# SS2D selective scan: the copy of dt * x into PSUM moves from TensorE to ScalarE, and an order edge behind it is taken out

## The chip, the cores and the metric

The kernel runs on one core of a Trainium2 chip. Its engines work side by side, each on its own queue in order: TensorE (PE in the profile, with its weight loads as PEld), VectorE (DVE), ScalarE (ACT) and GpSimd (POOL); SyncE (SP) issues nearly all the DMAs. The metric is the device time of one launch in microseconds (us).

## The reference, cut to what matters

The network has four layers on eight images of 56 x 56 positions with 128 channels, all in float32. Layers 0, 2 and 3 are deformable convolution blocks, which the change doesn't touch. Layer 1 is a VSS block: layer norm, an input projection, a depthwise convolution, the selective scan in two dimensions (SS2D), and an output projection with an MLP. The scan is the part that matters:

```python
x0 = xb.reshape(B, Di, L)                       # Di = 256, L = 3136
x1 = xb.transpose(0, 1, 3, 2).reshape(B, Di, L)
xs = jnp.stack([x0, x1, x0[..., ::-1], x1[..., ::-1]], axis=1)   # 4 directions
...
dt = jax.nn.softplus(dt + dt_projs_b[None, :, :, None])
A = -jnp.exp(A_logs).reshape(K, Di, N)          # N = 16 states a channel

def step(h, t):
    dt_t, u_t, B_t, C_t = t
    h = h * jnp.exp(dt_t[..., None] * A) + (dt_t * u_t)[..., None] * B_t[:, :, None, :]
    y = jnp.einsum('bkdn,bkn->bkd', h, C_t)
    return (h, y)
```

So each of 256 channels has 16 states; each state is a linear recurrence over 3136 positions, with the decay exp(dt * A) and the input (dt * x) * B; the output is the sum over the states of h * C.

## The kernel before, in words

`Vss.scans` works through 128 steps: 8 images, 4 directions and 4 chunks of 784 positions (SC). A step has 32 units. A unit puts 32 channels (TC) times 4 states (TS) on the 128 partitions and 784 positions along the free dimension. The units of a step go by channel group cg (8 of them) and, within one, by state group sg (0 to 3); four units thus share one channel group, which the text calls a group. There are 4096 units and 1024 groups.

A group's tile dt holds two planes, dt and dt * x, each repeated over the 4 states; one DMA fetches it (`fetch_dt`, three buffers). A unit then takes these steps:

- `decay`: ScalarE makes dA = exp(dt * A) from plane 0 of dt, into PSUM (two buffers).
- `inputs`: u = (dt * x) * B. For sg 0, 1 and 2 VectorE does it, and reads dt * x from dtu, a copy in PSUM. For sg 3 (`on_pool`) GpSimd does it, straight from plane 1 of dt, into up.
- VectorE scans: h from dA and u (three buffers of h). ScalarE copies the last column of h to st, the state with which the next chunk starts.
- GpSimd multiplies h by C into hc (six buffers).
- `add_sums`: TensorE sums hc over the states into acc in PSUM, two units at a time and three units later. `open_sums` and `close_sums` start acc and take it out through ScalarE.

`spread` makes the copy dtu: two matmuls of 392 columns with an identity matrix. It is called once for each group, in the unit with sg 1, for the group after it. dtu has one buffer, of two PSUM banks, so that the copy for the next group waits until VectorE has made this group's third u. `spread` keeps its last matmul in `self.last_spread`, and `add_sums` issues its matmuls inside `issue_after(self.last_spread)`: an order edge, by which these sums come behind the last copy in TensorE's queue.

Between the units, work of other stages is fed in as generators, some pieces at each unit: `prepare` makes dt, B and C of the next step, `input_stage` makes the projection and convolution of the next image, and `output_stage` the output projection and MLP of chunks already scanned. They use TensorE, ScalarE, VectorE and GpSimd, with one PSUM bank named misc. The code names what is issued and in which order; a planner of the framework then arranges each engine's queue by the costs that it assumes, and the arrangement differs from the order of the calls. The order of instructions in each queue is fixed in the program.

Of the kernel before, what the change touches and what calls it, by code (L numbers as in the profile page):

```python
# [120 lines left out]
SH = SC // 2  # L121
# [11 lines left out]
TC, TS = 32, 4  # L133
NCG, NSG = DI // TC, NST // TS
# [855 lines left out]
class Vss:  # L990
# [309 lines left out]
    def scans(self):  # L1300
        nc, w = self.nc, self.w
# [33 lines left out]
        def spread(at, t):  # L1335

            s, (cg, sg) = state[at], order[t]
            ps = s["dtu", cg] = self.pdtu.tile([128, 2, 512], F32, name="dtu", tag="dtu")
            for b in range(2):
                last = nc.tensor.matmul(ps[:, b, :SH], lhsT=self.net.ident, rhs=s["dt", cg][:, 1, SH * b : SH * (b + 1)], start=True, stop=True)  # L1340
            self.last_spread = last.ins

        def decay(at, t):
            (i, k, c), s, (cg, sg) = steps[at], state[at], order[t]
# [26 lines left out]

        def add_sums(at, group):
            acc = state[at]["acc"]
            with self.tc.issue_after(self.last_spread):
                for (cg, sg), hc in group:
                    for b in range(2):
                        r = 64 * b + TC * (cg % 2)
                        nc.tensor.matmul(acc[r : r + TC, :SH], lhsT=w["sum"], rhs=hc[:, SH * b : SH * (b + 1)], start=False, stop=sg == NSG - 1)  # L1378

        def close_sums(at, t):  # L1380
            (i, k, c), acc, (h, r) = steps[at], state[at]["acc"], place(t)
# [12 lines left out]
            if t == NT - 1:  # L1394
                state[at] = None
                if k == 2:
                    tasks.extend(self.output_stage(i, e) for e in (2 * c + 1, 2 * c))

        spread(*units[0])
        decay(*units[0])  # L1400
        inputs(*units[0])
        st = ready = None
        group, late = [], deque()
        zeros = self.zeros()
        for now, (at, t) in enumerate(units):
# [31 lines left out]
            if now + 1 < len(units):  # L1437
                decay(*units[now + 1])
                if not on_pool(units[now + 1][1]):
                    inputs(*units[now + 1])  # L1440

                if sg == NSG - 3 and now + 3 < len(units):
                    spread(*units[now + 3])
# [6 lines left out]
            if c != (NSC - 1 if forward else 0):  # L1450
                last = SC - 1 if forward else 0
                nc.scalar.copy(st[:, t : t + 1], hh[:, last : last + 1])  # L1452
            hc = self.work.tile([128, SC], F32, name="hc", tag="hc", bufs=6)
            nc.gpsimd.tensor_mul(hc, hh, s["c", sg])  # L1454
            group.append((order[t], hc))
            if t % 2:
                late.append((now + 3, add_sums, (at, group)))
                group = []
                if t % (2 * NSG) == 2 * NSG - 1:
                    late.append((now + 5, close_sums, (at, t)))  # L1460
# [83 lines left out]
```

## Time and profile before

| what | value |
|---|---|
| time, median of the runs | 18467.62 us (18457.31 to 18490.28) |
| span of the profiled execution | 18479.8 us |
| scan stage, from the first scan to the last | 2366 to 13800 us, 11434 us |
| busy in the stage: PE, DVE, ACT, POOL | 8638, 10264, 7052, 10454 us |
| granted TensorE clock: whole span, stage | 0.826, 0.86 |

The profiled execution's own time is known by its span alone, from its first to its last instruction, which is 12 us above the median of the runs. In the profile, a line such as L1340 is a line of the kernel; `dtu<-dt,ident` names the tile that is written and those that are read; `<-` behind an idle time names who ended it. Each of these matmuls stands as two records, so one call of `spread` gives four. Busy shares are best read inside the stage, since before and behind it other layers run.

### The profile page before, as it was taken

The page shows a single profiled execution, that of the slowest core. Times are in us where ns is not written, and L with a number is a line of the kernel's source. Part 1 is how long each engine was busy: PE and PEld are TensorE (multiplying, and loading weights), DVE is VectorE, ACT ScalarE, POOL GpSimd, SP SyncE. Part 2 cuts the span into 40 slices and gives each one's busy share as a digit, 9 for nine tenths or more (in the row PEclk, how much of TensorE's full clock was granted, in tenths as well). Part 3 has the DMA queues.
Part 4 walks back from the last instruction along what each step waited for, and adds up shares of the span by engine and source line. Part 5 has one row for each costly group of instructions (what it writes and reads, how often), then busy time and mean ns, then how long its engine had stood idle before and what let it go on. Part 6 is the DMA issues. An engine that isn't in the chain of part 4 may idle for free. (4 is left out here: it accounts for less than half of the span.)

```text
span 18479.8 us, 257190 instructions
## 1 busy us (share of the span) xinstructions
PE 13780.6 (75%) x89795; PEld 6844.2 (37%) x89795; DVE 15510.8 (84%) x18797; ACT 11145.4 (60%) x20690; POOL 11801.5 (64%) x6462
## 2 busy tenths in 40 slices
PE   5777787678678778678778768767665888577777
PEld 4555422222222222222222222222224666455555
DVE  8888379988988988988988898898985887688886
ACT  4666565566566566566566656656554666456666
POOL 2221089998998998998998998899981111222221
PEclk7878888889889889889888888888886888677777
DMA  7777444444443444344343443443433777577777
GB/s 215 205 210 200 122 158 160 162 158 148 142 149 137 146 147 140 140 150 139 140 150 136 143 152 135 143 150 136 147 122 110 196 198 198 143 204 204 201 204 175
DMA packets 1341779, 2961.90 MB, mean 160 GB/s; under 512 B 91168, under 2 KB 892132, under 8 KB 1325836
## 3 DMA queue, kind: packets, MB, share of 16 engines
q1 hardware_dynamic: 1340460, 2945.21, 51.4%
q8 instruction: 718, 11.76, 0.3%
q14 instruction: 601, 4.92, 0.1%
HBM read 2243.88 MB, written 866.92 MB: 168 GB/s over the span
## 5 line engine op out<-in xcount | busy, mean ns | idle before, releaser
L1454 POOL TENSOR_TENSOR hc<-h,c 128x784 f32<-128x784 f32 x4096 | 7560.9, 1873 | 764.2 <-DVE h L1449 534.4
L1449 DVE TENSOR_TENSOR_SCAN h<-dA,st,u 128x784 f32<-128x784 f32 x3072 | 5569.9, 1838 | 316.2 <-ACT dA L1346 182.3
L1346 ACT ACTIVATE dA<-dt,v_A 128x784 f32<-128x784 f32 x4096 | 3742.8, 915 | 719.1 <-DVE h L1449 717.8
L1356 DVE TENSOR_TENSOR u<-dtu,b 128x784 f32<-128x784 f32 x3072 | 2875.7, 957 | 559.9 <-PE dtu L1340 555.5
L1378 PE MATMUL acc<-hc,v_sum 128*32 128x392 f32 x16384 | 3222.3, 552 | 105.8 <-POOL hc L1454 105.6
L1340 PE MATMUL dtu<-dt,ident 128*128 128x392 f32 x4096 | 2105.1, 642 | 1512.1 <-issue 1102.6
L736 POOL TENSOR_TENSOR ay<-hat,om 112x756 f32<-112x756 f32 (+2 forms) x192 | 525.8, 2738 | 2750.0 <-ACT hat L727 2346.6
L1449 DVE TENSOR_TENSOR_SCAN h<-dA,st,up 128x784 f32<-128x784 f32 x1024 | 1876.7, 1833 | 242.4 <-POOL hc L1454 176.7
L1352 POOL TENSOR_TENSOR up<-dt,b 128x784 f32<-128x784 f32 x1024 | 1900.3, 1856 | 132.1 <-DVE h L1449 110.8
L807 ACT COPY st<-pt 128x448 f32<-128x448 f32 (+1 forms) x2240 | 1177.8, 542 | 1216.4 <-PE pt L805 1210.1
L1452 ACT COPY st<-h 128x1 f32<-128x1 f32 x3072 | 581.7, 189 | 2159.0 <-DVE h L1449 2150.5
L1340 PEld LDWEIGHTS dtu<-dt,ident 128*128 128x128 f32 x4096 | 862.0, 235 | 2564.6 <-issue 1672.2
L775 DVE TENSOR_TENSOR win<-win,patch 112x252 f32 (+2 forms) x3456 | 1695.4, 503 | 124.4 <-DVE win L775 34.2
L805 PE MATMUL pt<-ident,sw 112*128 112x112 f32 (+2 forms) x8960 | 1609.7, 310 | 199.1 <-DMA sw<-skew 198.8
L1378 PEld LDWEIGHTS acc<-hc,v_sum 128*32 128x32 f32 x16384 | 769.8, 117 | 2488.2 <-issue 1675.4
L766 POOL MEMSET win<- 128x1820 f32 (+2 forms) x384 | 630.1, 1646 | 1466.2 <-DMA skew<-win 1159.6
L821 PE MATMUL yps<-st,xw 128*32 128x48 f32 (+5 forms) x35840 | 1077.7, 245 | 397.6 <-ACT st L807 394.8
L805 PEld LDWEIGHTS pt<-ident,sw 112*128 112x128 f32 (+2 forms) x8960 | 1119.5, 161 | 485.6 <-DMA sw<-skew 166.9
L772 DVE TENSOR_TENSOR patch<-ay,hat 112x756 f32<-112x756 f32 (+2 forms) x1152 | 1221.3, 1066 | 22.5 <-POOL ay L736 19.5
L821 PEld LDWEIGHTS yps<-st,xw 128*32 128x32 f32 (+2 forms) x35840 | 757.0, 126 | 825.9 <-ACT st L807 476.1
L1112 PE MATMUL misc<-xn,v_tap 128*128 128x448 f32 x2016 | 867.3, 574 | 96.5 <-ACT xn L1146 61.2
L725 ACT ACTIVATE hat<-om,taps 112x252 f32<-112x252 f32 x1280 | 755.7, 729 | 287.1 <-DVE patch L772 273.4
(165 smaller groups left out, 19517.2 us busy)
## 6 DMA issues: line engine op xcount, KB each, us to landing
dt<-dds SPq DMA_DIRECT2D x1024, 784.0 KB
b<-rows SPq DMA_DIRECT2D x512, 392.0 KB
c<-rows SPq DMA_DIRECT2D x512, 392.0 KB
dds<-dd SPq DMA_DIRECT2D x256, 784.0 KB
sw<-skew SPq DMA_DIRECT2D x224, 812.0 KB
sw<-skew SPq DMA_DIRECT2D x224, 672.0 KB
sw<-skew SPq DMA_DIRECT2D x224, 588.0 KB
xw<-table SPq DMA_DIRECT2D x224, 320.0 KB
```

The lines of the kernel that those rows point to most:

```text
L772: nc.vector.tensor_mul(patch[:n], bcast(a, 3, KX), bcast(b, 2, KY))
L775: self.last_add = nc.vector.tensor_add(to, to, patch[:n, NCB * p : NCB * (p + 1)]).ins
L805: last = nc.tensor.transpose(ps[:m, n * g : n * (g + 1)], sw[:n, g, p : p + m], self.net.ident[:n, :n])
L807: nc.scalar.copy(st[:m], ps[:m, : G * n])
L821: self.nc.tensor.matmul(yps[CG * g : CG * (g + 1), t0:t1], lhsT=xw[:m, k + part, CG * g : CG * (g + 1)], rhs=st[:m, at + t0 : at + t1], st ...
L1340: last = nc.tensor.matmul(ps[:, b, :SH], lhsT=self.net.ident, rhs=s["dt", cg][:, 1, SH * b : SH * (b + 1)], start=True, stop=True)
L1346: nc.scalar.activation(da[:, :SC], s["dt", cg][:, 0], AF.Exp, scale=w["A"][:, k, NSG * cg + sg : NSG * cg + sg + 1])
L1352: nc.gpsimd.tensor_mul(u, s["dt", cg][:, 1], s["b", sg])
L1356: nc.vector.tensor_mul(halves[0], s["dtu", cg][:, :, :SH], halves[1])
L1378: nc.tensor.matmul(acc[r : r + TC, :SH], lhsT=w["sum"], rhs=hc[:, SH * b : SH * (b + 1)], start=False, stop=sg == NSG - 1)
L1449: nc.vector.tensor_tensor_scan(hh[:, ::step], dA[:, :SC][:, ::step], u[:, ::step], st[:, t : t + 1], ALU.mult, ALU.add)
L1454: nc.gpsimd.tensor_mul(hc, hh, s["c", sg])
```

## The change

`spread` no longer issues matmuls. One ScalarE copy writes both halves of dtu from plane 1 of dt. The copy is called at the same place and waits for the same things: the DMA of dt, and VectorE's last reading of dtu. `add_sums` issues its matmuls without the order edge, and `self.last_spread` is gone. Nothing else of the source is changed; the planner arranges the queues anew.

```diff
             ps = s["dtu", cg] = self.pdtu.tile([128, 2, 512], F32, name="dtu", tag="dtu")
-            for b in range(2):
-                last = nc.tensor.matmul(ps[:, b, :SH], lhsT=self.net.ident, rhs=s["dt", cg][:, 1, SH * b : SH * (b + 1)], start=True, stop=True)
-            self.last_spread = last.ins
+            nc.scalar.copy(ps[:, :, :SH], s["dt", cg][:, 1].rearrange("p (b e) -> p b e", b=2))
...
             acc = state[at]["acc"]
-            with self.tc.issue_after(self.last_spread):
-                for (cg, sg), hc in group:
-                    for b in range(2):
-                        r = 64 * b + TC * (cg % 2)
-                        nc.tensor.matmul(acc[r : r + TC, :SH], lhsT=w["sum"], rhs=hc[:, SH * b : SH * (b + 1)], start=False, stop=sg == NSG - 1)
+            for (cg, sg), hc in group:
+                for b in range(2):
+                    r = 64 * b + TC * (cg % 2)
+                    nc.tensor.matmul(acc[r : r + TC, :SH], lhsT=w["sum"], rhs=hc[:, SH * b : SH * (b + 1)], start=False, stop=sg == NSG - 1)
```

## The prediction

> **What bounds the kernel now.** I read the page first: its groups of instructions show that the five costliest rows belong to one stage, the selective scan. In each row, the number after the bar is busy time, then the mean ns of one; the second bar leads to the engine's idle time before these instructions and who ended it.
>
> ```profile
> span 18479.8 us, 257190 instructions
> ...
> L1454 POOL TENSOR_TENSOR hc<-h,c 128x784 f32<-128x784 f32 x4096 | 7560.9, 1873 | 764.2 <-DVE h L1449 534.4
> L1449 DVE TENSOR_TENSOR_SCAN h<-dA,st,u 128x784 f32<-128x784 f32 x3072 | 5569.9, 1838 | 316.2 <-ACT dA L1346 182.3
> L1346 ACT ACTIVATE dA<-dt,v_A 128x784 f32<-128x784 f32 x4096 | 3742.8, 915 | 719.1 <-DVE h L1449 717.8
> L1356 DVE TENSOR_TENSOR u<-dtu,b 128x784 f32<-128x784 f32 x3072 | 2875.7, 957 | 559.9 <-PE dtu L1340 555.5
> ...
> L1340 PE MATMUL dtu<-dt,ident 128*128 128x392 f32 x4096 | 2105.1, 642 | 1512.1 <-issue 1102.6
> ```
>
> The first and last scan of the timeline bound this stage: 2366 to 13800 us. The table of that stretch (span; then busy us per engine PE, PEld, DVE, ACT, POOL; granted clock; DMA share) reads:
>
> ```profile
> 2366.00:13800.00 11434.00, 8637.61 (x31300) 3030.12 (x31298) 10264.15 (x8600) 7051.73 (x13027) 10453.60 (x5761) 0.86 0.41 145
> ```
>
> POOL is busy 10453.6/11434 = 91.4%, DVE 89.8%, ACT 61.7%. POOL multiplies what DVE scans, so the two run in step, and an idle microsecond of DVE is lost unless POOL has work left over. 4096 units share the 11434 us, 2.79 us each. What DVE and POOL idle for, from the list of waits in that stretch:
>
> ```profile
> DVE u L1356 <- PE dtu L1340: 473.5, 258, 7.8
> DVE h L1449 <- ACT dA L1346: 234.3, 199, 4.2
> DVE h L1449 <- POOL hc L1454: 214.4, 165, 3.2
> ...
> POOL hc L1454 <- DVE h L1449: 534.4, 465, 8.4
> POOL hc L1454 <- PE acc L1378: 176.1, 121, 4.2
> ```
>
> The largest wait of DVE is the one for the copy that the change moves. (The page's row has 555.5 for it; I take the smaller 473.5, 258 times, which a count of DVE's gaps ahead of u in the trace repeats.) The timeline shows one such wait: DVE finishes u at 8020.75, the copy starts 0.10 us later, runs at half speed for 2.95 us, and DVE stood for 3.09 us.
>
> ```profile
> 8019.80 0.95 DVE L1356 TENSOR_TENSOR u<-dtu,b 128x784 f32<-128x784 f32 x1
> 8020.26 1.28 ACT L1218 ACT_TABLE_LOAD   x1
> ...
> 8020.85 2.95 PE L1340 MATMUL dtu<-dt,ident 128*128 128x392 f32 x4 [3.69 <-issue]
> ...
> 8023.84 0.97 DVE L1356 TENSOR_TENSOR u<-dtu,b 128x784 f32<-128x784 f32 x1 [3.09 <-PE dtu L1340]
> ```
>
> **What is removed.** Four matmul records per group of four units, 4096 in all, 2105 us of PE. dtu has one buffer, so a copy can begin only when the group's third u has ended, and the next group's first u needs it. Counted over the 1023 gaps between groups in the trace: TensorE starts the copy 1.12 us after that u on the mean (0.05 us where nothing is in its way), and takes 1.58 us in most groups, 2.95 us in about a third. In 153 of the late groups TensorE was busy with other matmuls when dtu came free (335 us of lateness), in 102 the copy itself was too long (129 us).
>
> **What is added, on ACT.** 1024 copies of 128x784. The trace has no copy of this shape from SBUF to PSUM. Nearest row: dA, 915 ns, the same source tile, elements and destination memory. From the other side: copies of 392 and 448 elements take 479 and 542 ns, a slope of 1.125 ns an element, so 920 ns; two copies of 392 would be 958. I take 915; the range 900 to 960 is worth under 50 us of ACT. 1024 x 0.915 = 937 us, which takes ACT from 7052 to 7989 us, 70% of the stage.
>
> **When the copy would be ready.** In the same gaps ACT becomes free 0.26 us after the third u has ended, on the mean. With 0.06 us for each of two handovers (the trace's shortest are 0.04 and 0.05), the copy is ready 0.26 + 0.12 + 0.915 = 1.30 us after that u; DVE reached the next u 4.08 us after it. Taken group by group, ACT would be late by 44 us in sum where TensorE was late by 464. Gain: 473 - 44, about **430 us**. Bounds: 473 if never late; nothing or less if the copy stands behind other work (below).
>
> **What it costs behind it on ACT.** The copy waits for DVE's u and then holds ACT for 0.92 us; queued behind it are the exponentials dA, which the scan needs, the st copies (needed one chunk later), and the small activations that free the one misc bank of PSUM. ACT was idle 1.96 us of the mean 4.08 us gap, which is the cover. Pushing the ACT records behind each third u by 0.975 us, and letting each idle stretch absorb its part, 179 dA end after their scan started: **122 us** in sum. Without any idle on ACT it would be all 937.
>
> **What TensorE loses and gains.** It waits for no u any more; the edge goes too, which held the sums behind the last copy. That is worth little: of the 176 us that POOL waited for sums (to get an hc buffer), a copy had run just before in 11 us only. [...]
>
> [...] In the 5 us behind each stall on dtu POOL is idle 16% of the time against 7% elsewhere: the excess is 154 us for 473 us of stall, a third. So one third is the floor of what a removed stall is worth and the whole its ceiling; since POOL cannot be over 100% and would be at 93% after it, I take four fifths.
>
> **Sum.** 430 - 122 - 90 = 218; times 0.8 is 175. Profiled span 18480 - 175 = 18305. The median shown, 18468, is 12 below that span, so **18,290**.
>
> **A planner** fills the queues, and it moved things. In the instruction order before, the next group's first u stands behind the group's last scan in 761 of 1024 groups, mostly with two scans between it and the third u. In the changed order that holds for 283; in 741 it stands ahead of the last scan, and in 446 of these one scan alone (1.84 us) lies between. A copy that is late thus holds that scan too. One scan still covers 1.30 us. On ACT the commonest order is two dA, copy, dA: the dA ahead (0.92 us) runs during the third u (0.96 us) and ends as the copy may start.
>
> DMA: SP issues the same transfers; dt's wait moves from PE to ACT. No late copy before was found waiting with PE idle, so dt had landed; if the issue moved later, ACT would stand for it.
>
> **Rivals.**
> 1. *POOL hides it.* One third of the net, with the dA cost at twice its estimate: (430 - 244 - 90)/3 = 32, so 18,435, within 0.2% of before (about what a measurement of this kernel can tell from no change). For: 91.4% POOL, 214 us of DVE waiting for it. Against: POOL waits 534 us for the scan, more than the reverse.
> 2. *ACT becomes the late one; slower.* Where the planner left one scan, a background activation (0.48 to 0.58 us) or a table load with its activation (1.28 + 1.51 us) ahead of the copy uses up the slack, and the scan behind u stands too. With a mean lateness x over the 741 groups the sum is 473 - 741x - 212; it turns at x = 0.35 us. At 0.65 us it is -220: 18,690. For: ACT already makes DVE wait 234 us at 62% busy, and goes to 70%. Against: it is free 0.26 us after u.
> 3. *More than forecast.* The full ceiling, 430 less 0 to 100, from a stage where sums run early: 18,050. For: DVE and POOL wait for the scan chain far more than for each other. Against: POOL's own 10454 us, which would then be 95% of the stage.
>
> **Chances.** Forecast (18,290, own range 18,130 to 18,430) 0.44; rival 3 0.12; rival 1 0.12; rival 2 0.32. Faster 0.56, same 0.11, slower 0.33 (a hundredth of rival 1 falls to slower). The range leaves out the lower half of rival 3 and the upper third of rival 2: 18,000 to 18,720.
>
> **What would show it.** Right: the wait of u for dtu falls from 473 to under 100 us; a copy row x1024 on ACT near 915 ns; ACT near 70%; DVE's wait for dA near 350 us; PE in the stage near 6500 us or more if colder; clock under 0.86. Wrong: waits of u for ACT near or over 473, dA waits over 500, POOL's wait for sums doubled, or POOL at 93% with the stage unchanged.

## The result

The changed kernel takes 18,697.12 us (median, 18,690.64 to 18,704.1) against 18,471.8 us before: a ratio of 1.0118, with a 95% interval of 1.0106 to 1.0131. The forecast was 18,290 us and faster. The time lies inside the range given, but on the other side of the kernel before.

The page of the changed kernel has these groups (busy time, mean ns of one; then idle time before, and who ended it):

```profile
span 18689.1 us, 248742 instructions
...
L1451 POOL TENSOR_TENSOR hc<-h,c 128x784 f32<-128x784 f32 x4096 | 7543.9, 1862 | 1104.2 <-DVE h L1446 927.2
L1446 DVE TENSOR_TENSOR_SCAN h<-dA,st,u 128x784 f32<-128x784 f32 x3072 | 5580.4, 1839 | 825.5 <-ACT dA L1344 626.1
L1375 PE MATMUL acc<-hc,v_sum 128*32 128x392 f32 x16384 | 4241.9, 628 | 1969.5 <-POOL hc L1451 1953.0
...
L1354 DVE TENSOR_TENSOR u<-dtu,b 128x784 f32<-128x784 f32 x3072 | 2898.1, 955 | 260.1 <-ACT dtu L1339 252.5
```

The new copy, from the list of one line's instructions in the stage:

```profile
L1339 ACT COPY dtu<-dt 128x784 f32<-128x784 f32 x1023 | 828.1, 810 | 44.1 <-DVE u L1354 43.5
```

It is cheaper than the 915 ns taken, and it hardly waits. The stage from the first scan to the last now runs from 2360 to 14004 us; its table (PE, PEld, DVE, ACT, POOL, clock):

```profile
2360.00:14004.00 11644.00, 8089.28 (x27210) 2298.91 (x27210) 10271.00 (x8601) 7744.60 (x14052) 10440.55 (x5763) 0.76 0.41 143
```

The stage grew by 210 us, from 11,434; the rest of the span stayed. DVE and POOL are as busy as before, so the 210 us are waits. The list of DVE's waits in the stage:

```profile
DVE h L1446 <- ACT dA L1344: 682.7, 448, 5.8
DVE u L1354 <- ACT dtu L1339: 174.2, 70, 8.2
DVE h L1446 <- POOL hc L1451: 155.9, 155, 3.3
DVE bn_st L1069 <- PE misc L1173: 99.0, 39, 8.0
DVE xt L1198 <- PE misc L1195: 65.3, 20, 5.9
...
DVE xt L1227 <- PE misc L1224: 43.3, 22, 6.6
```

The wait for dtu fell from 473 to 174 us, as forecast in kind. What came in its place is dA: 683 us for 234. The other riser is the misc tiles, 99 + 65 + 43 = 208 us for 45 + 31 + 20 = 96.

Why is dA late, on an engine that is busy 67% of the stage? The waits of TensorE's queue in the stage show what is new, first before, then after:

```profile
PE acc L1378 <- POOL hc L1454: 105.2, 123, 2.0
```

```profile
PE acc L1375 <- POOL hc L1451: 1952.7, 1618, 6.5
```

TensorE now stands 1953 us for hc. Counted over the 4096 units in the trace, the median time from the end of hc to the start of its sums was 7.3 us before and is 0.5 us after; 1913 units have their sums start within 0.2 us of hc, for 176 before. The sums come to the head of TensorE's queue before hc is there, and what lies behind them stands too. The timeline of the changed kernel shows one whole case (start, duration, engine, instruction, idle before):

```profile
9256.20 1.84 DVE L1446 TENSOR_TENSOR_SCAN h<-dA,st,up 128x784 f32<-128x784 f32 x1
...
9257.45 1.50 PE L1251 MATMUL misc<-xb,v_xproj 128*40 128x392 f32 x2
...
9260.32 1.52 PE L1375 MATMUL acc<-hc,v_sum 128*32 128x392 f32 x4 [1.38 <-POOL hc L1451]
...
9261.77 1.53 PE L1251 MATMUL misc<-xb,v_xproj 128*40 128x392 f32 x2
...
9263.34 0.48 ACT L1253 COPY dbl<-misc 40x392 f32<-40x392 f32 x1 [6.96 <-PE misc L1251]
9263.72 0.91 ACT L1344 ACTIVATE dA<-dt,v_A 128x784 f32<-128x784 f32 x1
...
9264.72 1.85 DVE L1446 TENSOR_TENSOR_SCAN h<-dA,st,u 128x784 f32<-128x784 f32 x1 [4.05 <-ACT dA L1344]
```

TensorE does half of a background matmul, then its next instruction is a sum whose hc isn't ready; the second half of the background work starts at 9261.77. ScalarE's next instruction is the copy of that work's result, so ScalarE stands idle for 6.96 us; TensorE's wait of 1.38 us for hc and the 1.52 us of the sums lie in them. Behind the copy stands dA, which needs nothing from TensorE, and behind dA the scan: VectorE idles 4.05 us.

Counted over the stage in the trace, ScalarE stood for TensorE while TensorE stood for hc during 341 us in the changed kernel, and never before. The case above is the smaller kind: 101 us are ahead of ScalarE's work on background results in misc, 240 us ahead of its copies of acc (y and out), which need the late sums themselves. The delay then lasts: ScalarE is idle for TensorE in only 116 of the 683 us that VectorE waits for dA, and busy in nearly all the rest, with what had queued up. In 585 of the 683 us the last idle stretch of ScalarE ahead of the late dA was one that TensorE ended; in the kernel before it was 190 of 234.

### The profile page after: what moved, and what is told of

The parts are those of the page before. It is cut to its first block, busy times and chain, and to the rows that moved or that the text cites. A ratio compares the mean times of both kernels' runs of the same rounds, so it can differ in the third digit from the quotient of the medians.

```text
span 18689.1 us, 248742 instructions
## 1 busy us (share of the span) xinstructions
PE 13232.9 (71%) x85699; PEld 6116.5 (33%) x85699; DVE 15517.0 (83%) x18797; ACT 11834.0 (63%) x21714; POOL 11796.5 (63%) x6462
## 5 line engine op out<-in xcount | busy, mean ns | idle before, releaser
L1451 POOL TENSOR_TENSOR hc<-h,c 128x784 f32<-128x784 f32 x4096 | 7543.9, 1862 | 1104.2 <-DVE h L1446 927.2
L1446 DVE TENSOR_TENSOR_SCAN h<-dA,st,u 128x784 f32<-128x784 f32 x3072 | 5580.4, 1839 | 825.5 <-ACT dA L1344 626.1
L1375 PE MATMUL acc<-hc,v_sum 128*32 128x392 f32 x16384 | 4241.9, 628 | 1969.5 <-POOL hc L1451 1953.0
L1368 PE MATMUL acc<-y,ident 128*64 128x392 f32 x1536 | 621.8, 822 | 482.2 <-ACT y L1386 317.1
L1386 ACT COPY y<-acc 64x392 f32<-64x392 f32 x768 | 575.7, 750 | 472.2 <-PE acc L1375 464.8
```

What stands on the lines that cost most here:

```text
L1446: nc.vector.tensor_tensor_scan(hh[:, ::step], dA[:, :SC][:, ::step], u[:, ::step], st[:, t : t + 1], ALU.mult, ALU.add)
```

## The experiments

Four theories. *Edge* (order): without the edge the sums stand too early in TensorE's queue, and the chain above follows. *ScalarE*: the copies' own time delays dA. *Clock*: TensorE with less to do runs more at half clock (5685 us of the stage for 3199 before, by the clock records of the two traces, which hold full and half clock alone). And the *copy* as such: what it is there for.

**The edge alone, with TensorE's copies.**

```diff
-            with self.tc.issue_after(self.last_spread):
-                for (cg, sg), hc in group:
+            for (cg, sg), hc in group:
```

> One part alone: TensorE keeps the copy, only the order edge between copy and sums is taken out. Edge theory (without the edge the sums come to stand early in TensorE's queue, TensorE stands there for GpSimd's hc with the small matmuls of the background behind it, ScalarE stands for those, and dA is late): slower, 18,600 to 18,800 us; DVE's wait for dA over 450 us and TensorE's wait for hc over 1000 us in the stage. ScalarE theory (the 0.81 us of each copy in ScalarE's queue delays dA): as before, 18,470 within 40, dA wait near 234. Clock theory (TensorE without the copies falls to half clock more often): as before too, since the matmuls are all there.

Measured: 19,391.72 us, ratio 1.0499 (1.0482 to 1.0517), far more than any theory said. TensorE's wait for hc is 1841 us, as large as in the changed kernel. Here the sums hold up the copies themselves:

```profile
DVE u L1356 <- PE dtu L1340: 1344.5, 633, 10.0
DVE h L1448 <- ACT dA L1346: 332.2, 246, 4.7
PE acc L1377 <- POOL hc L1453: 1840.9, 1308, 6.9
```

The edge is worth 919 us to the kernel before. The clock (0.85 in the stage, for 0.86) and ScalarE (no copies) can't explain it. The edge theory had the sign and the wait for hc, and missed where it lands: on dtu, 1345 us for 473, more than on dA, whose 332 us stay under the 450 forecast.

**The sums pinned behind all earlier TensorE work.**

```diff
-                    nc.tensor.matmul(acc[r : r + TC, :SH], ...)
+                    self.tc.keep_in_program_order(nc.tensor.matmul(acc[r : r + TC, :SH], ...))
```

> The changed kernel, with every matmul of the sums pinned behind all that the code has issued to TensorE before it: the sums can't overtake the background matmuls, and ScalarE still copies. Edge theory: most of the loss and more comes back, 18,250 to 18,450 us, dA wait under 350 us. ScalarE theory: stays at 18,650 to 18,750 us with a dA wait over 550. Clock theory: stays near 18,700 while the granted clock of the stage stays near 0.76.

Measured: 18,764.42 us, 1.0163 (1.0146 to 1.018): a miss for the edge theory as it was put. TensorE's wait for hc falls from 1953 to 1087 us only, and ScalarE still stands for TensorE during 249 us of it. The other end shows now as well: POOL waits 597 us for sums to free hc, for 97 in the changed kernel, and DVE waits 535 us for POOL.

```profile
DVE h L1446 <- ACT dA L1344: 642.3, 336, 7.7
DVE h L1446 <- POOL hc L1451: 534.7, 314, 5.9
POOL hc L1451 <- PE acc L1375: 597.4, 257, 8.3
```

So keeping the sums behind earlier work is not the remedy by itself, and this run doesn't tell the theories apart: its time is near that of the ScalarE theory.

**More TensorE work in the changed kernel.**

```diff
+                    nc.tensor.matmul(acc[r : r + TC, SH:512], lhsT=w["sum"], rhs=hc[:, SH * b : SH * b + 512 - SH], start=False, stop=False)
                     nc.tensor.matmul(acc[r : r + TC, :SH], ...)
```

> The changed kernel with one matmul of 120 columns more beside each matmul of the sums, into columns of acc that nobody reads: about 4096 x 2 x 2 x 0.15 = 2460 us more of TensorE, against the 2105 us that the change took away. Clock theory: the stage's clock rises from 0.76 to 0.85 or over and the time falls to 18,450 to 18,600. Edge theory: 18,690 to 18,900, the clock up and the waits of ScalarE for TensorE as they were or longer. ScalarE theory: 18,650 to 18,750.

Measured: 18,783.2 us, 1.0168 (1.0151 to 1.0185), at a granted clock of 0.83 in the stage. Most of the clock came back (0.76 to 0.83, for 0.86 before) and the time didn't: it rose by 86 us, and dA's wait is 762 us. That is what the edge theory forecast; the clock theory's time is missed. The added matmuls take time of their own in the same queue (TensorE is busy 8588 us of the stage, for 8089), so the clock alone isn't measured here.

**ScalarE's time alone, in the kernel before.**

```diff
             da = s["dA", t] = self.pda.tile([128, 1024], F32, name="dA", tag="dA")
+            if sg == 0:
+                nc.scalar.copy(da[:, :SC], s["dt", cg][:, 1])
```

> The kernel before, edge and TensorE copies as they were, with one ScalarE copy of 784 elements from plane 1 of dt into the group's first dA tile, just ahead of the exponential that overwrites it: ScalarE's price alone, 1024 x 0.81 = 829 us. ScalarE theory: 18,650 us or more, dA wait over 550 us. Edge and clock theories: at most 18,560 us, the dA wait up by 100 to 150 us as the 122 us of the prediction.

Measured: 18,850.54 us, 1.0207 (1.019 to 1.0224). The ScalarE theory's time was met, its dA wait of over 550 us was not; the others missed both. The stage grew by 371 us, 0.36 us for each of the 1024 copies, when they stand straight ahead of the exponential.

```profile
DVE h L1451 <- ACT dA L1348: 437.8, 367, 4.5
```

That is 204 us more than before. Of the rest about 97 us are waits for dtu (571 for 473, leaving out one of 82 us ahead of the first scan), so the 371 us are not dA's alone. By its time this run spoke for the ScalarE theory; the next one has as many copies in another place.

**The edge kept where ScalarE copies.** An order edge on TensorE needs an instruction there, so a matmul of 8 columns into unread columns of acc marks the place. It reads the group's third u and waits for it, as the old copy did.

```diff
                     spread(*units[now + 3])
+                    if self.acc is not None:
+                        self.last_mark = nc.tensor.matmul(self.acc[TC : 2 * TC, SH : SH + 8], lhsT=w["sum"], rhs=s["u", t + 1][:, :8], start=False, stop=False).ins
...
         def add_sums(at, group):
             acc = state[at]["acc"]
-            for (cg, sg), hc in group:
+            with self.tc.issue_after(self.last_mark) if self.last_mark else nullcontext():
+                for (cg, sg), hc in group:
```

> The changed kernel with the order edge kept: a matmul of 8 columns into unread columns of acc, which reads the group's third u and so waits for it as the old copy did, stands at the copy's place in TensorE's queue, and the sums are issued behind the last such matmul. Order theory (the edge that was taken out costs most of the loss also where ScalarE copies): 18,250 to 18,500 us, TensorE's wait for hc far under 1953 us, dA wait under 400. ScalarE theory (the copies' own time in ScalarE's queue is what delays dA): 18,600 to 18,750 us with a dA wait over 550 us, whatever TensorE's waits do.

Measured: 18,325.3 us, 0.9914 (0.9897 to 0.993). It beats both kernels: 153 us under the runs of before beside it (18,478.58), 372 us under the changed kernel (the runs of before beside the two differ by 7 us). Its granted clock in the stage is 0.77, nearly that of the changed kernel, and ScalarE does the same copies. This is the run that decides. Its stage, and the waits of DVE and of TensorE in it:

```profile
2355.00:13641.00 11286.00, 7705.83 (x29254) 2491.41 (x29254) 10274.78 (x8601) 7764.46 (x14052) 10414.28 (x5763) 0.77 0.42 147
```

```profile
DVE h L1450 <- ACT dA L1344: 394.6, 254, 6.2
DVE h L1450 <- POOL hc L1455: 175.5, 180, 3.4
DVE u L1354 <- ACT dtu L1339: 141.7, 67, 5.0
```

```profile
PE acc L1444 <- DVE u L1354: 1356.6, 515, 7.6
PE acc L1368 <- ACT y L1387: 570.0, 257, 6.1
PE acc L1376 <- POOL hc L1455: 271.0, 269, 4.4
```

TensorE still stands, 1357 us for u at the mark, but what ScalarE needs is not behind it: only 1.4 of these 1357 us fall on a wait of ScalarE for TensorE, and 15 of the 271 us for hc, where the changed kernel has 341. The sum of all of ScalarE's waits for TensorE over the stage was 1284 us before, 1775 in the changed kernel, and is 1144 here (and 2276 without the edge where TensorE copies). The median from hc to its sums is back at 5.0 us. The mark seems to add a small wait of its own: 56 us of VectorE ahead of u, put down to TensorE's sums.

The planner arranged the other queues anew too. In VectorE's, the next group's first u stands ahead of the group's last scan in 771 of 1023 groups here and in 740 in the changed kernel. So this part of VectorE's order, which the prediction feared for, hardly differs between the two.

**Without the copies into st, in the changed kernel and in the one before.** Both leave out the state that a chunk hands to the next.

```diff
-            if c != (NSC - 1 if forward else 0):
-                last = SC - 1 if forward else 0
-                nc.scalar.copy(st[:, t : t + 1], hh[:, last : last + 1])
```

> The changed kernel without the 3072 copies of the scan's last column into st, so that each chunk starts from zero: leaves out 581 us of ScalarE and its waits for the scan. ScalarE theory: DVE's wait for dA falls under 350 us and the time to 18,350 to 18,550. Order theory: dA waits stay over 550 us and the time within 80 us of 18,697.

> The same left out of the kernel before: the control for the run without st copies where ScalarE copies. ScalarE theory: gains less than there, 18,380 to 18,480 us, since ScalarE had room. Order theory: gains as much as there, within 60 us.

Measured: 18,587.49 us, 1.0058 (1.0041 to 1.0075) for the changed kernel, 18,445.59 us, 0.9982 (0.9974 to 0.9989) for the one before. ScalarE's time is worth more in the changed kernel (110 us against 33), but VectorE's wait for dA stays at 631 us:

```profile
DVE h L1446 <- ACT dA L1344: 631.2, 388, 7.0
```

The records of these copies overlap those of other ScalarE work: its busy time in the stage fell by 292 us (7745 to 7452), not by the 581 us that they sum to. Freeing that much doesn't mend dA. Neither theory's numbers were met in full; ScalarE's load is a part, not the cause of the 1.2%.

**No copy at all.**

```diff
-            ps = s["dtu", cg] = self.pdtu.tile([128, 2, 512], F32, name="dtu", tag="dtu")
-            nc.scalar.copy(ps[:, :, :SH], ...)
...
-                nc.vector.tensor_mul(halves[0], s["dtu", cg][:, :, :SH], halves[1])
+                nc.vector.tensor_mul(u, s["dt", cg][:, 1], s["b", sg])
```

> The changed kernel with no copy at all: VectorE makes u from plane 1 of dt in SBUF, as GpSimd does for up. What the copy as such costs: with u at 0.96 us and hc at 1.87 us as before, the wait for dtu gone and dA at about 234 us, 18,000 to 18,300 us. If the two engines slow each other down where both read SBUF, u, scan or hc grow in duration, and at 0.3 us a unit the time is over 18,900.

Measured: 20,614.08 us, 1.1156 (1.1138 to 1.1175), the second branch of what was expected. The groups of its stage:

```profile
L1448 POOL TENSOR_TENSOR hc<-h,c 128x784 f32<-128x784 f32 x4095 | 9223.3, 2272 | 985.4 <-DVE h L1443 832.9 <-DVE bn_mv L1070 78.5 <-PE acc L1372 30.6
...
L1351 DVE TENSOR_TENSOR u<-dt,b 128x784 f32<-128x784 f32 x3071 | 5280.1, 1736 | 13.1
```

u takes 1736 ns for 955 in the changed kernel, hc 2272 for 1862, and the scan, which reads dA from PSUM, is unchanged at 1834 (1839 in the changed kernel). The 29 u of this stage that had no GpSimd instruction beside them took 965 ns on the mean, for 1743 of the rest, which speaks for the meeting of the two engines as what costs. Without the copy the kernel is 1917 us slower than the changed kernel.

**The clock where the order is good.** The version with the edge kept, and the added matmuls beside the sums (112 columns).

```diff
+                        nc.tensor.matmul(acc[r : r + TC, SH + 8 : 512], lhsT=w["sum"], rhs=hc[:, SH * b : SH * b + 504 - SH], start=False, stop=False)
```

> The version with ScalarE's copy and the order edge kept, with one matmul of 112 columns more beside each matmul of the sums, into columns of acc that nobody reads. It asks what TensorE's clock is worth where the order is good: that version took 18,325 us at a granted clock of 0.77 in the stage. Clock theory (the 90 us of the prediction): the stage's clock rises to 0.83 or over and the time falls to 18,200 to 18,290 us. If the clock is worth nothing beside the queue: 18,310 to 18,450 us, not below the version without the added matmuls.

Measured: 18,489.66 us, 1.0002 (0.9992 to 1.0012). The clock rose from 0.77 to 0.82 and the kernel became 164 us slower than without the added matmuls, over both ranges. Their own time is in that (TensorE is busy 8348 us of the stage, for 7706), so the clock's worth isn't isolated; but no gain from it is seen in either order.

**The sums called one unit later.**

```diff
-                late.append((now + 3, add_sums, (at, group)))
+                late.append((now + 4, add_sums, (at, group)))
```

with the opening and closing of acc at now + 6 for now + 5.

> The changed kernel without an edge, but with the sums, and the opening and closing of acc around them, called one unit later in the code. If the planner's order follows readiness and not the order of the calls, the sums stay early in TensorE's queue: 18,640 to 18,760 us, TensorE's wait for hc over 1500 us. If a later call is enough to let the background matmuls pass, as the edge did: 18,300 to 18,500 us and TensorE's wait for hc under 1000 us.

Measured: 18,740.12 us, 1.0138 (1.0121 to 1.0155), the first branch of what was expected.

```profile
PE acc L1375 <- POOL hc L1451: 1770.0, 1453, 6.9
```

A call that comes one unit later doesn't do what the edge did.

## Why the prediction was wrong, step by step

**The step that failed** is in "What TensorE loses and gains": "the edge goes too, which held the sums behind the last copy. That is worth little". It has no term in the sum, on the strength of one count: in how much of POOL's 176 us for sums a copy had just run (11 us). That count asks what the edge delayed. It doesn't ask what the edge kept out of the way: the background matmuls ran ahead of sums whose hc was not ready. With the edge kept the same ScalarE copy takes 18,325 us, without it 18,697: the step was worth +372 us, and with TensorE's copies +919. The prediction's own sign of being wrong, dA waits over 500 us, came with it (683). The row that should have warned is TensorE's wait for hc, 105 us before, with sums that started 7.3 us after their hc: the edge was the reason that nothing stood there.

**The gain on dtu** was right in kind, too large in size: 430 us forecast, 299 measured in the changed kernel, 332 with the edge kept. Its copies were late in 70 and 67 groups. The copy itself was cheaper than taken (0.81 us for 0.915), but ScalarE was not as free: the copy was ready 2.39 us after the third u on the mean in the changed kernel and 1.90 us with the edge kept, for the 1.30 forecast, and within 1.30 us in 444 and 602 of 1023 groups. So the lateness was 174 and 142 us where 44 was forecast.

**The cost on dA**, 122 us, was mis-sized for the changed kernel (448 measured), but near for the version with the edge (160). The 122 was meant as the cost of ScalarE's time in its new place, and 160 is the nearest measurement of that; the other 288 us go when the edge is kept, so they belong to the failed step. In another place, ahead of the exponential, as many copies put 204 us on dA and 371 us on the stage.

**The clock.** The granted clock fell, as forecast, from 0.86 to 0.76. The 90 us put on it were the author's estimate, and no run shows that term. What the runs showed in its place: in the changed kernel POOL's wait for sums fell from 176 to 97 us; the misc waits rose by 112, but with the edge kept, at a clock of 0.77, they are 31 + 14 + 35 = 80 us, fewer than the 96 before. Where matmuls were added the clock rose, from 0.76 to 0.83 and from 0.77 to 0.82, and the time rose with it, by 86 and 164 us. What lowered the clock in the changed kernel is not shown.

**The sum** for what the ScalarE copy does by itself was 175 us of gain; with the edge kept it is 153, and the forecast of 18,290 is 35 us from that version's time. In part that nearness is luck: the gain on dtu was taken 98 us too large and the cost on dA 38 us too small, while the 90 us for the clock were not seen and a fifth was taken off for POOL. The gain came with the busy time of POOL, the busiest engine of the stage, about as before (10,414 us for 10,454). What was forecast was one half of the change.

**The rivals.** Rival 2 named 18,690 us, close to the time measured, by a mechanism that did not happen: it had copies late by 0.65 us over 741 groups, 481 us of waiting for dtu. That wait is 174. Of its reasons "ScalarE goes to 70%" holds (67%). No rival had the edge. The planner was looked at for where VectorE's u stands; TensorE's queue, where the edge works, was not compared in the same way.

What stays open: why pinning the sums behind earlier work didn't help. One reading is that the pinned sums let no later background work pass while they wait; it is not shown. The trace shows both ends (TensorE still 1087 us for hc, POOL 597 us for sums), but no run moved the two apart. And the mark is not the edge itself: it waits for u, as the old copy did, so the runs show that this edge and wait together are worth 372 us, not each one's share.

## What to carry to other kernels

An order edge has two sides: besides what it holds up, ask what runs in the gap that it keeps open, above all where a planner may put early in a queue what is not yet ready. When a step moves to another engine, an order edge tied to the old instruction goes with it, so the edge must be priced, and kept if needed, apart from the move. An engine that stands in its queue while not the bound can stop the bound through a third engine: here TensorE stood 1953 us for GpSimd, ScalarE stood for TensorE during 341 us of them, and VectorE stood 683 us for ScalarE.

## What was not expected of the hardware

VectorE's product u takes 957 ns on the mean with one operand in PSUM and one in SBUF (the kernel before), and 1736 ns with both in SBUF (the run with no copy), where GpSimd's product hc grew from 1873 to 2272 ns. The 29 u of that run without a GpSimd instruction beside them took 965 ns on the mean; the rest took 1743 ns on the mean and up to 6333 ns. By what mechanism they grow is not shown. A ScalarE copy of 128x784 from SBUF to PSUM took 810 ns, where the exponential over the same elements takes 914.
